# Order of the eight sampling matmuls in a deformable-convolution network: group by group instead of half by half

## The chip, the cores and the metric

The kernel runs on one core of a Trainium2 chip. The metric is device time in microseconds (us) of one execution of the whole program, four convolution layers over a batch of four images. The runs of the kernel before took 7743.75, 7739.45 and 7736.22 us, with a median of 7739.45 us.

## The reference, cut to what matters

The input is a tensor of 4 images, 256 channels, 64 x 64 pixels, in 32-bit floats. Four layers follow one another, each a group normalisation, a block, and a residual sum. The change lies in the first layer, a deformable convolution. There every pixel and every one of 4 channel groups (64 channels each) has 9 sampling points, whose places come from the data. Each point reads four neighbouring pixels (the corners) and weighs them bilinearly, and a softmax over the 9 points weighs the points:

```python
return tap(x0, y0, (1 - wx) * (1 - wy)) + tap(x0 + 1, y0, wx * (1 - wy)) + tap(x0, y0 + 1, (1 - wx) * wy) + tap(x0 + 1, y0 + 1, wx * wy)
...
samp = _grid_sample(img, sg)
mr = mask.reshape(n, H * W, G, P).transpose(0, 2, 1, 3).reshape(n * G, 1, H * W, P)
dout = (samp * mr).sum(-1).reshape(n, G * GC, H * W).transpose(0, 2, 1).reshape(n, H, W, C)
dout = jnp.einsum('nhwc,oc->nhwo', dout, outproj_w) + outproj_b
```

So for each pixel and group, 36 weighted rows of 64 channels are added up (9 points, 4 corners), and the result goes through a 256 x 256 projection.

## The kernel before

**Stages.** `run` (line 1178) works image by image. While image n is sampled, other work of earlier images stands beside it: for image 0 the convolutions and offsets of the images after it, for image 1 the feed-forward part and the linear attention of image 0, for images 2 and 3 also the last two layers of images 0 and 1. The tail after the sampling finishes what is left. A helper, `beside` (line 1194), takes one sampling round at a time and then lets the other generators advance by their share of cost. Under `manual_schedule` (line 1217) PE, DVE, ACT and POOL execute their instructions in the order in which the Python code issues them, so this interleaving is the order on each engine's queue.

**A sampling round.** `sample` (line 556) walks an image in rounds of 14 pixels (`RP`), with 9 points each, so that 126 of 128 partitions are points; there are 293 rounds an image and 1172 in all. A table in memory, `tab`, holds for each group and place a row of 64 channels for two lines, so that 256 consecutive floats give all four corners of a point: two halves of 128 floats, one for each x, and in each half two corners of 64 channels.

- `gathered` (line 596) allocates `g`, a tile of 128 partitions x 4 groups x 256 floats with 7 buffers. POOL issues four indirect DMAs (line 600), one for each group, which fetch 128 rows of 256 floats by the indices in `sl`.
- Eight matmuls follow (lines 605 to 608). For group i and half x the stationary operand is a slice of `wm` with 32 columns (2 corners x 16 pixel slots) and the moving operand is the half of `g` with 128 columns. The result goes to partitions 32i to 32i+31 of `acc` in PSUM, so each group has 32 columns of the PE array and 32 PSUM partitions to itself. The half x=0 starts the sum and the half x=1 is added to it.
- `weigh` (line 585) makes `wm` for four rounds on DVE, from weights and a mask that has each point's pixel.
- Two rounds share a half of the `acc` bank. When both are done, `moved` (line 610, ACT) copies it to SBUF, `turned` (line 614, PE) transposes it, and `spread` (line 619, ACT) writes it to `dT`. At the end of a block of 16 rounds come `project` (line 636, PE), `add` (DVE) and `finish` (ACT). They are held in `later` and issued some rounds afterwards, ahead of that round's own gathers and matmuls.

The first matmul of each group waits for that group's gather; the first of a round waits also for `wm` and for the copy that frees `acc`. The last matmul of a round tells the others that the round is done: POOL, which reuses the `g` buffer seven rounds later, ACT for `acc`, and DVE for `wm`.

**Another place with column tiles.** In the first image's convolution, `projected` (lines 385 to 393) also writes parts of PSUM's partitions: its loop over h chooses partitions 0 to 63 or 64 to 127, and the loop over the two contraction halves k stands inside it (line 392).

Of the kernel before, what the change touches and what calls it, by code (L numbers as in the profile page):

```python
# [23 lines left out]
G, PT = 4, 9  # L24
# [47 lines left out]
class Net:  # L72
# [483 lines left out]
    def sample(self, n, ssum):  # L556
# [39 lines left out]
        def gathered(sl, wm, acc, r):  # L596
            r4, acc = r % WR, acc[:, r % UR * P:(r % UR + 1) * P]
            g = self.gp.tile([P, G, 256], F32, name="g", bufs=7)
            for i in range(G):
                nc.gpsimd.indirect_dma_start(  # L600
                    out=g[:, i, :], out_offset=None, in_=table,
                    in_offset=bass.IndirectOffsetOnAxis(ap=sl.bitcast(I32)[:, r, i:i + 1], axis=0))


            for x in range(2):
                for i in range(G):
                    nc.tensor.matmul(acc[32 * i:32 * i + 32, :], wm[:, r4, 4 * i + 2 * x:4 * i + 2 * x + 2, :],  # L607
                                     g[:, i, x * P:(x + 1) * P], start=x == 0, stop=x == 1)

# [47 lines left out]
        for i, (b, r) in enumerate(order):  # L657
            for f in later.pop(i, ()):
                f()
            sl, rounds = blocks[b]  # L660
            if r % UR == 0:
                acc = next(accs)
            gathered(sl, wm, acc, r)
            if r == 0 and b + 1 < len(BLOCKS):
                load(b + 1)
            ends = r + 1 == len(rounds)
            if r % WR == 0:
                if r + WR < len(rounds):
                    nxt = weigh(b, r + WR)
                elif b + 1 < len(BLOCKS):  # L670
                    nxt = weigh(b + 1, 0)
            if r % UR == UR - 1 or ends:
                unit = rounds[r - r % UR:r + 1]
                todo = [partial(moved, acc, len(unit), i), partial(turned, len(unit), i), partial(spread, unit, b, i)]

                todo = [(i + 1 + j + (j == 2 and r < UR), f) for j, f in enumerate(todo)]
                if ends:
                    todo += [(i + 4 + m + j, partial(f, b, m)) for m in range(KT) for j, f in enumerate((project, add, finish))]
                for j, f in todo:
                    later.setdefault(j, []).append(f)  # L680
            if r % WR == WR - 1 or ends:
                wm = nxt
            yield 1
# [659 lines left out]
```

## Time and profile before

| What | us |
|---|---|
| median of the runs | 7739.45 |
| span of the profiled execution | 8805.8 |
| of this: before the first sampling round | 139 |
| sampling of the four images (1172 rounds) | 7192 |
| after the last sampling round | 1475 |
| PE busy with matmuls | 5993.9 |
| DVE busy | 5173.3 |
| POOL busy | 5152.4 |
| ACT busy | 2183.8 |
| matmuls of line 607, busy in all | 1034.8 |

The profiled execution has a longer span than the runs without a profile took. PE is TensorE (matmuls), PEld its weight loads, DVE is VectorE, ACT ScalarE, POOL GpSimd. A row of the profile that groups instructions has the line of the kernel, the engine, the operation, the tiles written and read, the count, the busy time and the mean duration of one in ns, and the idle time of the engine ahead of them with what ended it. A matmul in 32-bit floats appears as two array instructions, each with a weight load. Matmuls overlap, so the busy time of a group is the time in which at least one of them ran, and not the count times the mean. In a row of a stretch, the columns are the stretch, its length, the busy time of PE, PEld, DVE, ACT and POOL with instruction counts, the granted share of the TensorE clock, the share of the DMA engines and GB/s.

### The profile page before, as it was taken

How to read it: one execution, taken by the hardware profiler on the slowest of the kernel's cores; microseconds unless marked ns; L12 is line 12 of the kernel's file. 1: busy time of each engine (PE TensorE's matmuls, PEld its weight loads, DVE VectorE, ACT ScalarE, POOL GpSimd, SP SyncE). 2: the span in 40 equal slices, each digit the busy share in tenths (PEclk: the TensorE clock that was granted, in tenths of full speed). 3: DMA queues.
4: the chain of work that ended last, by engine and by line, in shares of the span. 5: the costliest groups of instructions: out<-in, count | busy, mean ns of one | idle time of the engine just before them, and what ended most of it. 6: DMA issues, size and time to landing. Idle time of an engine off the chain costs nothing. (4 is left out here: it accounts for less than half of the span.)

```text
span 8805.8 us, 95736 instructions
## 1 busy us (share of the span) xinstructions
PE 5993.9 (68%) x36532; PEld 3575.6 (41%) x36532; DVE 5173.3 (59%) x6409; ACT 2183.8 (25%) x4899; POOL 5152.4 (59%) x4950
## 2 busy tenths in 40 slices
PE   4454554448744446688876677888766778986899
PEld 2222222224323322244544443345544433664477
DVE  5444443443466667424777776227777772599834
ACT  1111111112211112122223222222222222465524
POOL 2666666566666666666666656666666661376410
PEclk7676766669866667799988888898878888998999
DMA  6454454444433334444443344444434343220131
GB/s 172 127 155 124 141 154 118 125 145 145 153 105 105 110 105 129 127 130 138 134 135 110 112 121 136 142 134 132 136 115 117 114 118 99 69 74 29 48 98 53
DMA packets 759050, 1042.27 MB, mean 118 GB/s; under 512 B 362432, under 2 KB 472128, under 8 KB 757056
## 3 DMA queue, kind: packets, MB, share of 16 engines
q0 software_dynamic: 225024, 614.77, 24.3%
q1 hardware_dynamic: 533568, 421.39, 16.4%
q8 instruction: 289, 4.73, 0.2%
q14 instruction: 169, 1.38, 0.0%
HBM read 867.08 MB, written 168.69 MB: 118 GB/s over the span
## 5 line engine op out<-in xcount | busy, mean ns | idle before, releaser
L600 POOL DMA_INDIRECT g<-tab,sl x4688 | 4618.5, 985 | 2687.8 <-issue 1224.2
L178 DVE SCALAR_TENSOR_TENSOR agg<-pad,vec,agg 128x1024 f32<-128x1024 f32 x2280 | 2933.5, 1287 | 61.9
L607 PE MATMUL acc<-g,wm 128*32 128x128 f32 x18752 | 1034.8, 333 | 1907.8 <-ACT at L612 1273.7
L607 PEld LDWEIGHTS acc<-g,wm 128*32 128x32 f32 x18752 | 566.8, 128 | 2411.7 <-ACT at L612 1446.1
L1048 PE MATMUL ps<-xd,w 128*128 128x256 f32 x3072 | 752.7, 396 | 51.3 <-issue 37.8
L591 DVE TENSOR_TENSOR wm<-con,sl 128x1024 f32<-128x1024 f32 (+1 forms) x296 | 357.7, 1209 | 711.9 <-remote 533.5
L1048 PEld LDWEIGHTS ps<-xd,w 128*128 128x128 f32 x3072 | 595.1, 199 | 175.0 <-issue 86.0
L632 ACT COPY dT<-dp 64x112 f32<-64x112 f32 x1176 | 285.9, 243 | 1043.7 <-remote 544.3
L742 PE MATMUL ps<-x2f,f 128*128 128x512 f32 x1024 | 499.2, 636 | 19.1 <-issue 7.7
L817 PE MATMUL ps<-xr,qw 128*128 128x512 f32 x768 | 472.0, 746 | 22.1 <-issue 11.1
L727 DVE SCALAR_TENSOR_TENSOR hm<-ps,vec,lk 128x512 f32<-128x512 f32 x256 | 190.8, 750 | 492.9 <-ACT lk L744 405.5
L752 PE MATMUL ps<-hm,f 128*128 128x512 f32 x1024 | 467.1, 605 | 0.9 <-DVE hm L727 0.9
L612 ACT COPY at<-acc 128x256 f32<-128x256 f32 (+1 forms) x588 | 218.3, 371 | 986.3 <-remote 753.2
L999 POOL TENSOR_TENSOR xd<-xp 128x640 f32<-128x640 f32 x64 | 79.4, 1268 | 492.6 <-ACT xp L1011 298.3
L640 PE MATMUL po<-dT,ow 128*128 128x224 f32 (+1 forms) x1216 | 326.1, 419 | 45.4 <-issue 19.3
L617 PE MATMUL dp<-ident,at 128*128 128x128 f32 x1172 | 284.1, 330 | 106.6 <-ACT dT L632 61.0
L865 ACT COPY kt<-pt 128x512 f32<-128x512 f32 x256 | 149.4, 584 | 829.3 <-remote 403.8
L744 ACT ACTIVATE lk<-ps,low 128x512 f32<-128x512 f32 x256 | 174.0, 687 | 666.0 <-PE ps L742 512.1
L1147 PE MATMUL s<-ph,th 128*128 128x512 f32 x512 | 290.2, 672 | 62.5 <-ACT kt L865 15.9
L640 PEld LDWEIGHTS po<-dT,ow 128*128 128x128 f32 x1216 | 265.5, 233 | 113.8 <-issue 68.9
L1167 PEld LDWEIGHTS ps<-gt,pT 128*128 128x128 f32 x2048 | 276.0, 213 | 70.8 <-issue 46.1
L194 POOL TENSOR_TENSOR ak<-ak,m 128x1024 f32<-128x1024 f32 x96 | 228.1, 2376 | 130.6 <-ACT m L193 126.7
(243 smaller groups left out, 8022.0 us busy)
## 6 DMA issues: line engine op xcount, KB each, us to landing
g<-tab,sl POOLq DMA_INDIRECT x4688
x<-x SPq DMA_DIRECT2D x128, 512.0 KB
xr<-x SPq DMA_DIRECT2D x96, 512.0 KB
tab<-xo SPq DMA_DIRECT2D x192, 128.0 KB
x<-in_x SPq DMA_DIRECT2D x32, 512.0 KB
y<-yc SPq DMA_DIRECT2D x32, 512.0 KB
x2f<-x SPq DMA_DIRECT2D x32, 512.0 KB
xyf<-x SPq DMA_DIRECT2D x32, 512.0 KB
```

Of the source, the lines that this page charges most:

```text
L178: nc.vector.scalar_tensor_tensor(to, s, wt, acc, ALU.mult, ALU.add)
L591: nc.vector.tensor_tensor(wm[:, 0:nu], self.con("own").unsqueeze(1).unsqueeze(1).to_broadcast(sh), sl[:, r:r + nu, G:].unsqueeze(3).to_bro ...
L600: nc.gpsimd.indirect_dma_start(out=g[:, i, :], out_offset=None, in_=table, in_offset=bass.IndirectOffsetOnAxis(ap=sl.bitcast(I32)[:, r, i: ...
L607: nc.tensor.matmul(acc[32 * i:32 * i + 32, :], wm[:, r4, 4 * i + 2 * x:4 * i + 2 * x + 2, :], g[:, i, x * P:(x + 1) * P], start=x == 0, st ...
L617: nc.tensor.transpose(dp[u][:, v].rearrange("p g s o -> p (g s o)"), at[u][:, v], self.ident)
L632: nc.scalar.copy(dT[b][hs, :, q0:q0 + m * (v1 - v0)].rearrange("p g (v o) -> p g v o", o=m), dp[u][hs, v0:v1, :, s, 0:m].rearrange("p v g ...
L640: nc.tensor.matmul(po[m][:, 0:np_], self.ow[:, k, m * P:(m + 1) * P], dT[b][:, k, 0:np_], start=k == 0, stop=k == G - 1)
L742: nc.tensor.matmul(ps, f1[:, k, m * P:(m + 1) * P], x2[:, k], start=k == 0, stop=k == KT - 1)
L752: nc.tensor.matmul(ps, f2[:, k, m * P:(m + 1) * P], hm[:, k], start=k == 0, stop=k == 4 * KT - 1)
L817: nc.tensor.matmul(ps, qw[:, k, m * P:(m + 1) * P], x[:, k], start=k == 0, stop=k == KT - 1)
L1048: nc.tensor.matmul(ps[:, e], w[:, k, t, 2 * half + e, m * P:(m + 1) * P], v[:, 2 * half + e, k, t:t + 8], start=i % 6 == 0, stop=i % 6 == 5)
L1147: nc.tensor.matmul(s[i], tv[:, 4 * b + j], ph[:, i * 512:(i + 1) * 512], start=True, stop=True)
```

## The change

The two loops around the eight matmuls of a round change places. Before, the four groups' first halves are issued and then the four groups' second halves; now both halves of group 0 are issued, then both of group 1, and so on. Operands, destinations and the start and stop flags stay as they are, and so do the gathers ahead of the loops.

```diff
-            for x in range(2):
-                for i in range(G):
+            for i in range(G):
+                for x in range(2):
                     nc.tensor.matmul(acc[32 * i:32 * i + 32, :], wm[:, r4, 4 * i + 2 * x:4 * i + 2 * x + 2, :],
                                      g[:, i, x * P:(x + 1) * P], start=x == 0, stop=x == 1)
```

## The prediction

> **What bounds the kernel now.** I read the span and clock first, then the stretches by image, the costliest groups, and the matmuls of line 607 one by one.
>
> ```profile
> core 0: 8805.8 us, clock 0.809
> ```
>
> The profiled execution took 8805.8 us, 1066.4 us (14%) more than the median of the runs shown, 7739.45. Part of the surplus can be seen: there are stretches in which no arithmetic engine works, such as this one, the columns being PE, PEld, DVE, ACT and POOL.
>
> ```profile
> 990.90:1001.00 10.10, 0.00 (x0) 0.00 (x0) 0.00 (x0) 0.00 (x0) 6.45 (x7) 0.65 0.45 133
> ```
>
> Such holes are no part of the change, so I use the profile for durations of single instructions and add the result to the median; I don't scale it by the span.
>
> The sampling of the four images fills 139 to 7331 us. By image:
>
> ```profile
> 139.00:1913.00 1774.00, 839.98 (x6645) 481.31 (x6646) 782.49 (x1036) 248.35 (x689) 1162.29 (x1170) 0.66 0.48 137
> 1913.00:3667.00 1754.00, 1036.69 (x6813) 547.54 (x6814) 1053.20 (x1056) 339.92 (x869) 1160.62 (x1172) 0.74 0.42 123
> 3667.00:5487.00 1820.00, 1367.42 (x8673) 819.04 (x8672) 1147.21 (x1372) 453.97 (x1108) 1144.32 (x1172) 0.87 0.44 128
> 5487.00:7331.00 1844.00, 1387.29 (x8814) 827.11 (x8813) 1153.10 (x1382) 459.89 (x1121) 1147.28 (x1172) 0.86 0.43 125
> ```
>
> PE is busy 47, 59, 75 and 75% of an image, DVE 44 to 63%, yet all four images take nearly the same time. What they share is POOL: 1172 gathers each.
>
> ```profile
> L600 POOL DMA_INDIRECT g<-tab,sl x4688 | 4618.5, 985 | 2687.8 <-issue 1224.2
> L607 PE MATMUL acc<-g,wm 128*32 128x128 f32 x18752 | 1034.8, 333 | 1907.8 <-ACT at L612 1273.7
> POOL g L600 <- PE acc L607: 494.3, 201, 23.2
> ```
>
> A gather starts 1.25 us after the one before (0.95 us and 0.30 of issue in the timeline), so a round of four needs 5.0 us of POOL. The 1172 rounds take 7192/1172 = 6.1 us each in the profile. If only the sampling were shorter in the unprofiled runs, it would be (7739.45 - 139 - 1475)/1172 = 5.2 us, an estimate that puts POOL at its pace nearly throughout. PE is the nearest second: 1387/293 = 4.7 us a round in the last image. So PE's time in a round counts in part: where POOL waits for PE to free a buffer (494 us), or where all wait behind PE's queue.
>
> **The round itself.** 18752/1172 = 16 array instructions for 8 matmuls, two for each. Counts of matmuls begun in one burst, by windows that end at 4005.572, .579, .586, .592, .704, .706 and 4006.10:
>
> ```profile
> L607 PE MATMUL acc<-g,wm x1: 297/297/297, 4005.6 to 4005.6; 128*32 128x128 f32 x1
> L607 PE MATMUL acc<-g,wm x2: 297/297/297, 4005.6 to 4005.6; 128*32 128x128 f32 x2
> L607 PE MATMUL acc<-g,wm x3: 297/297/297, 4005.6 to 4005.6; 128*32 128x128 f32 x3
> L607 PE MATMUL acc<-g,wm x4: 297/297/297, 4005.6 to 4005.6; 128*32 128x128 f32 x4
> L607 PE MATMUL acc<-g,wm x5: 272/297/297, 4005.6 to 4005.7; 128*32 128x128 f32 x5
> L607 PE MATMUL acc<-g,wm x16: 272/273/297, 4005.6 to 4005.9; 128*32 128x128 f32 x16
> ```
>
> Four begin within 20 ns, 7 ns apart; then nothing begins until 134 ns after the first. So the four groups run side by side on their 32 columns in four waves. Whether that survives the new order is the whole question.
>
> The kernel has a line where neighbours already share their columns: line 392 in `projected`, part of the first image's convolution, whose loops (388 to 392) put k innermost. Two matmuls, hence four array instructions, go to columns 0 to 63 before the first one for columns 64 to 127. If a matmul waited for all before it, the second column half would begin about three waves late. One burst of it, in windows from 955.44 that end at 955.453 and .466 (the one to .464 still has one matmul, the one to .4515 none), and in the timeline:
>
> ```profile
> L392 PE MATMUL ps<-iw,yc x1: 430/430/430, 955.5 to 955.5; 128*64 128x256 f32 x1
> L392 PE MATMUL ps<-iw,yc x2: 430/430/430, 955.5 to 955.5; 128*64 128x256 f32 x2
> ...
> 955.45 2.00 PE L392 MATMUL ps<-iw,yc 128*64 128x256 f32 x16
> ```
>
> The first two begin 11 to 14.5 ns apart, I take 13, and all 16 take 2.00 us where one alone is recorded with 0.38 to 0.43: they go in pairs from the first wave on. The array works off its column tiles independently, whatever stands between them in the program. The 13 ns are two matmuls at 6.7 ns, the same 6.7 ns that one matmul costs between groups on line 607.
>
> **What the Trainium skill says.** "TensorE: Matmul & The Clock Gate", Part 3, The mechanism, says that matmuls on different array tiles overlap with about 4 ns between starts; here it is 7 ns for a matmul of two instructions, of the same size. It also says that matmuls start and end strictly in program order. Line 392 doesn't agree: in strict order its second column half could not begin 13 ns after the first. "TensorEngine Tiling (Array Packing)", Key Properties, says that tiles operate independently and that a change of tiling mode drains the array; the first fits line 392, and the second the timeline, where the 128x512 matmul after the burst begins at 4006.14, 0.57 us after the burst's start and only after its last wave. The table at the top of the first page gives TensorE a queue of 64; a round has 32 instructions, loads counted. No trace here shows that limit.
>
> **The change, part by part.** Removed and added: nothing; the same 9376 matmuls with the same operands, flags and accumulation per group.
>
> Moved: matmul (group 1, half 0) goes from second to third place, group 2 from third to fifth, group 3 from fourth to seventh; the second halves move forward. No DMA, no queue but PE's. Within a column tile the order is the same as before, so a tile's own chain stays: starts at 0, 134, 243, 352 ns (the waves at 109 ns after the first).
>
> Cost: the four tiles begin one matmul apart now (0, 7, 13, 20 ns) and two matmuls apart after (0, 13, 27, 40 ns), by line 392's 13 ns. The last tile ends 20 ns later, and the next 128-row work waits for it. 1172 x 20 ns = 23.4 us on PE's queue. Two rounds without PE work in between might pay a little more, since a tile's queue is then full when the next group comes; I put that at under 2 us in all.
>
> The gather waits sit on each group's first matmul. A late group 3 leaves four instructions in its tile after its landing, 352 ns to the last start, before and after; groups 0 to 2 would have more behind them. PE waits for landings 46 us in 49 cases, so a gain is bounded by about 49 x 0.25 = 12 us (two waves each, an estimate) and is near nothing, since the tiles run in parallel anyway. The evacuation (ACT, line 612) and POOL wait for the round's end alone: 20 ns later.
>
> How much of the 23.4 us shows: at most PE's share of the images, (0.47 + 0.59 + 0.75 + 0.75)/4 = 0.64, giving 15 us, or all of it if PE's queue sets the pace in unprofiled runs, 23; at least what POOL waits for line 607, 494/7192 = 0.07, 2 us. What hides the rest is POOL's 5.0 us a round; were it gone, all 23 would show. I take 0.4, between 0.07 and 0.64 and nearer the upper since the last two images are so close to both limits: +9.4 us, 7739.45 + 9.4 = 7749, +0.12%.
>
> **Rivals.** About 0.2% (15.5 us) is what a measurement of this kernel can tell from no change.
>
> *A shared hold-back (slower).* In line 392 the pairs are even for four waves only; what holds in a queue of two 64-column tiles needn't hold for four tiles of 32. If the array holds back only some eight instructions for all tiles together, three waiting for each of groups 0 and 1 and two for group 2 fill it, and group 3 begins a wave late: about 115 ns a round, 1172 x 0.115 = 135 us on PE. It decides from the point where PE's round passes POOL's; with the same 0.4: +54 us, 7793. For it: it is not excluded. Against it: line 607 itself has at least seven waiting after the first wave, and a shared store weighted by columns would be odd.
>
> *Strict order (slower).* Only the last of a group's four instructions overlaps the next group: last start at 4 x 352 + 3 x 7 = 1429 ns against 372, +1.06 us a round, 1239 us on PE. Images 3 and 4 then need 4.7 + 1.06 = 5.8 us a round of PE against 5.2; with half of it showing +620 us, 8360. Line 392 speaks against it.
>
> *Earlier start of the second halves (faster).* Worth at most the 12 us above, 7734 with half of it. More than 0.2% would need the engines' phases to shift favourably too.
>
> **How the numbers follow.** The lag case has 0.74 (0.42 within 0.2%, 0.29 slower since the lag may show in full or with a few us of shifted phases on top, 0.03 faster); the shared hold-back 0.10 (0.09 slower, 0.01 within); strict order 0.06, slower; the earlier start 0.10 (0.06 faster, 0.04 within). So faster 0.09, same 0.47, slower 0.44. The likeliest case alone spans 7735 to 7765 (0 to 23 us, and the 4 us by which the runs before stray). The range reaches down to 7728 for the earlier start and up to 7795 for the shared hold-back; strict order and the far tails are left out.
>
> **What would show it.** Right: in the changed kernel's burst the first wave begins at 0, 13, 27, 40 ns, the last start is 392 ns after the first instead of 372, line 607's PE busy time grows by about 20 us, and rounds, waits and clock are otherwise the same. Group 3's first start at 130 ns or more speaks for the shared hold-back; a burst of over 1.4 us for strict order. Wrong in its second half: bursts as foretold, but the time off by over 25 us, which would put the cause outside the array.

## The result and the profile after

The changed kernel took 7768.87 us (median of 7 runs, 7761.36 to 7771.16), the kernel before 7744.24 us (7 runs, 7736.22 to 7747.75): ratio 1.003, interval 1.002 to 1.004, or 24.6 us more. The forecast was 7749.0 with a range of 7728 to 7795. So the time lies in the range, on the slower side, 19.9 us over the forecast.

The first profile of the kernel before, on which the prediction rests, has a span of 8805.8 us. Later runs on one chip, called chip 13 here, take about 8830 us for this program instead of 7740; the first profile has such a time, and stretches in which no arithmetic engine works (halts). Which chip it came from is not known. The profile after has a span without that surplus, so it must be set beside an execution of the kernel before on a chip that shows none (chip 9, `before_null` below). The page of the changed kernel, with its span and three of the costliest groups of the sampling:

```profile
span 7768.7 us, 95736 instructions
...
L600 POOL DMA_INDIRECT g<-tab,sl x4688 | 4610.9, 984 | 1667.7 <-issue 1316.2
...
L607 PE MATMUL acc<-g,wm 128*32 128x128 f32 x18752 | 1507.9, 310 | 1025.7 <-ACT at L612 513.0
...
L591 DVE TENSOR_TENSOR wm<-con,sl 128x1024 f32<-128x1024 f32 (+1 forms) x296 | 357.5, 1208 | 404.3 <-PE acc L607 385.9
```

The same page of the kernel before, on chip 9:

```profile
span 7735.2 us, 95736 instructions
...
L600 POOL DMA_INDIRECT g<-tab,sl x4688 | 4594.5, 980 | 1652.0 <-issue 1311.6
...
L607 PE MATMUL acc<-g,wm 128*32 128x128 f32 x18752 | 1323.0, 319 | 1106.2 <-DMA g<-tab,sl 575.1
```

Two things are to be seen. POOL's gathers, which the change doesn't touch, are busy 16.4 us longer in all, and POOL's idle time before them grew by 15.7 us; together that is the 33.5 us between these two spans, to within 2 us. What grew in the idle time is POOL's wait for the matmuls of line 607 to free a `g` buffer: 116.0 us in 96 waits in the kernel before, 133.5 us in 100 waits in the changed one. And the matmuls of line 607 are busy 184.9 us longer, not the 20 that were foretold. In the kernel before, PE's largest wait ahead of them is for landing gathers (575.1 us), of which the first profile showed 46.

The burst itself is as foretold. Counts of matmuls begun in one burst of the changed kernel, whose first start is at 4007.994 us, in windows that end at 4008.003, .0125, .0400, .1350 and .3900 (the window to .1200 still has four):

```profile
L607 PE MATMUL acc<-g,wm x1: 297/297/297, 4008.0 to 4008.0; 128*32 128x128 f32 x1
L607 PE MATMUL acc<-g,wm x2: 297/297/297, 4008.0 to 4008.0; 128*32 128x128 f32 x2
L607 PE MATMUL acc<-g,wm x4: 297/297/297, 4008.0 to 4008.0; 128*32 128x128 f32 x4
L607 PE MATMUL acc<-g,wm x5: 273/297/297, 4008.0 to 4008.1; 128*32 128x128 f32 x5
L607 PE MATMUL acc<-g,wm x16: 272/273/297, 4008.0 to 4008.4; 128*32 128x128 f32 x16
```

Read at full resolution, the sixteen begin at 0, 14, 27, 40, then 134, 147, 160, 174, 243 and so on to 392 ns. Four groups run side by side in four waves, two matmuls' issue apart: the lag of 20 ns at the end is there. The question is whether it is what costs 24.6 us; 1172 rounds of 20 ns would be 23.4 us, nearly the same.

### The profile page after: what moved, and what is told of

The parts are those of the page before. It is cut to its first block, busy times and chain, and to the rows that moved or that the text cites. A ratio compares the mean times of both kernels' runs of the same rounds, so it can differ in the third digit from the quotient of the medians.

```text
span 7768.7 us, 95736 instructions
## 1 busy us (share of the span) xinstructions
PE 6126.8 (79%) x36532; PEld 3735.2 (48%) x36532; DVE 5164.4 (66%) x6409; ACT 2187.4 (28%) x4899; POOL 5144.8 (66%) x4950
## 5 line engine op out<-in xcount | busy, mean ns | idle before, releaser
L600 POOL DMA_INDIRECT g<-tab,sl x4688 | 4610.9, 984 | 1667.7 <-issue 1316.2
L607 PE MATMUL acc<-g,wm 128*32 128x128 f32 x18752 | 1507.9, 310 | 1025.7 <-ACT at L612 513.0
L607 PEld LDWEIGHTS acc<-g,wm 128*32 128x32 f32 x18752 | 878.1, 120 | 1689.6 <-ACT at L612 725.7
L1048 PE MATMUL ps<-xd,w 128*128 128x256 f32 x3072 | 708.8, 383 | 7.5 <-DVE x L1028 3.3
L1048 PEld LDWEIGHTS ps<-xd,w 128*128 128x128 f32 x3072 | 574.6, 192 | 108.4 <-issue 30.3
L742 PE MATMUL ps<-x2f,f 128*128 128x512 f32 x1024 | 482.4, 619 | 4.2 <-ACT f L717 3.9
L817 PE MATMUL ps<-xr,qw 128*128 128x512 f32 x768 | 445.6, 711 | 21.5 <-issue 7.5
L617 PE MATMUL dp<-ident,at 128*128 128x128 f32 x1172 | 263.3, 310 | 69.8 <-ACT dT L632 69.7
L640 PE MATMUL po<-dT,ow 128*128 128x224 f32 (+1 forms) x1216 | 287.1, 386 | 23.3 <-DVE yb L644 11.4
L742 PEld LDWEIGHTS ps<-x2f,f 128*128 128x128 f32 x1024 | 192.3, 195 | 232.7 <-issue 220.1
L752 PEld LDWEIGHTS ps<-hm,f 128*128 128x128 f32 x1024 | 188.4, 190 | 223.9 <-issue 222.4
```

Of the source, the lines that this page charges most:

```text
L600: nc.gpsimd.indirect_dma_start(out=g[:, i, :], out_offset=None, in_=table, in_offset=bass.IndirectOffsetOnAxis(ap=sl.bitcast(I32)[:, r, i: ...
L617: nc.tensor.transpose(dp[u][:, v].rearrange("p g s o -> p (g s o)"), at[u][:, v], self.ident)
L640: nc.tensor.matmul(po[m][:, 0:np_], self.ow[:, k, m * P:(m + 1) * P], dT[b][:, k, 0:np_], start=k == 0, stop=k == G - 1)
L742: nc.tensor.matmul(ps, f1[:, k, m * P:(m + 1) * P], x2[:, k], start=k == 0, stop=k == KT - 1)
L752: nc.tensor.matmul(ps, f2[:, k, m * P:(m + 1) * P], hm[:, k], start=k == 0, stop=k == 4 * KT - 1)
L817: nc.tensor.matmul(ps, qw[:, k, m * P:(m + 1) * P], x[:, k], start=k == 0, stop=k == KT - 1)
```

## The experiments

Two theories stood at first. *Lag*: PE's queue is 20 ns later a round, and part of it shows. *Order of landing*: the cost comes in the rounds in which PE waits for gathers. Such rounds are nearly all in the first two images, while PE is busiest in the last two. So the order was changed in some images only, beside fresh runs of the kernel before.

### The kernel before again (chip 13)

No edit; two runs, one with each of the next two sets.

> The kernel before once more, for an undisturbed profile: a span of about 7742 us beside 7744 us of time. All theories expect bursts of line 607 with first starts at 0, 7, 13, 20 ns and a last start at 372 ns. If POOL sets the pace of images 0 and 1, their bursts wait for landings (as the profile of the changed kernel shows) and those images take the same time as there, to 5 us; if PE's queue sets the pace of images 2 and 3, these are shorter here by 10 to 25 us.

> The kernel before a third time, to read it beside the profile of the changed kernel (7768.7 us). If this chip gives 7744 us: images 0 and 1 wait for landings in some 210 and 140 rounds as there, and last as long as there (1521 and 1533 us, to 5 us); images 2 and 3 are shorter by 10 to 12 us in all if only their 586 rounds show 20 ns each, and all four are shorter by about 6 us each if every round shows it. If this chip gives 8830 us: image lengths of about 1800 us as in the last look.

8834.59 and 8806.52 us. On this chip the kernel before has medians of 8829.73 and 8824.11 us in the two sets. The first profile (8805.8) is of this kind. What is compared on chip 13 therefore has some 1090 us of other time in it.

### The new order in two of the four images (chip 13)

```diff
-            for x in range(2):
-                for i in range(G):
+            for i, x in [(i, x) for i in range(G) for x in range(2)] if n < 2 else [(i, x) for x in range(2) for i in range(G)]:
```

This is `first_images`; `last_images` has `n > 1` instead of `n < 2`. `first_again` and `last_again` repeat them.

> Group order in the sampling of images 0 and 1 only, the order of before in images 2 and 3. Lag on PE's queue in every round alike: half of the change, +12 us (7756). Lag that shows only where PE doesn't wait for gathers: images 0 and 1 wait for them in most rounds, so 0 to +5 us (7744 to 7749). A cost that arises while PE waits inside a burst for a gather, and not from the lag: nearly all of it here, +20 to +25 us (7767).

> Group order in images 2 and 3 only. Lag in every round alike: +12 us (7756). Lag that shows only where PE doesn't wait for gathers: 586 rounds x 20 ns = 12 us from the array, and nearly the whole 24.6 us of the change if it has no other place, so +12 to +25 us. A cost of waits inside bursts: 0 to +5 us.

> Group order in images 0 and 1 only, again, for a chip without the long halts. Lag in every round alike: +12 us over the kernel before. Lag only where PE doesn't wait for gathers: 0 to +5 us. A cost of waits inside bursts: +20 to +25 us.

> Group order in images 2 and 3 only, again. Lag in every round alike: +12 us. Lag only where PE doesn't wait for gathers: +12 us, and up to +25 us if the 24.6 us of the change all lie here. A cost of waits inside bursts: 0 to +5 us.

Ratios to the kernel before: first images 0.9992 (0.9984 to 1.0) and 1.0004 (0.9993 to 1.0015); last images 1.001 (0.9999 to 1.0021) and 1.0002 (0.999 to 1.0014). The repeats don't confirm the first pair, and all four are within 0.1% of no change. For the first images the intervals allow -14 to 0 and -6 to +13 us, so the 20 to 25 us expected of a cost that arises in waits did not show on this chip. That says little of the other chip: in `before_third` only 49 rounds of images 0 and 1 have starts over more than 1 us, against 334 in `before_null`, so the rounds in which PE waits for landings are nearly absent here. The changed kernel itself was not run on chip 13.

### Groups in pairs (chip 13)

```diff
-            for x in range(2):
-                for i in range(G):
+            for i, x in [(i, x) for h in (0, 2) for x in range(2) for i in (h, h + 1)]:
```

> Groups 0 and 1 half by half, then groups 2 and 3 half by half. If a start costs one matmul's issue (6.7 ns) for each matmul ahead of it in the program, the first starts of the four groups are at 0, 7, 27 and 33 ns and the last start at 385 ns, 13 ns later than before; the time is then 13/20 of the change's, +16 us (7760). If a shared queue or the array's program order held anything back, group 2 would start a wave (110 ns) late and the time would be over +60 us. A cost of waits inside bursts alone has no reason to follow 13/20.

Ratio 1.0012 (1.0002 to 1.0022), about 2 to 19 us more. In the bursts without a wait the first starts of the groups are at 0, 7, 27 and 33 ns and the last start is at 385 ns (medians), as 6.7 ns for each matmul ahead in the program give. The model of the burst holds for a third order. The time agrees with the 16 us that the lag was expected to cost, but doesn't single it out.

### Two rounds' matmuls issued together (chip 13)

If PE's queue sets the pace, one change of tile shape fewer in each pair of rounds should show. The matmuls of two rounds that share a half of `acc` are issued after the second round's gathers, in the old order:

```diff
-            gathered(sl, wm, acc, r)
+            held.append((gathered(sl, r), wm, acc, r))
...
+                while held:
+                    sampled(*held.pop(0))
```

The last two lines stand where the half of `acc` is full or the block of rounds ends; `sampled` has the two loops of before.

> The order of before within a round, but the matmuls of the two rounds that share an acc half are issued together after the second round's gathers, so that PE changes between 128x32 and 128x128 half as often. In the profile of the changed kernel a change costs 93 ns on the way in (522 against 429 ns between starts) and 94 ns on the way out (203 against 109): 187 ns saved for about 470 pairs that were apart. If PE's queue sets the pace in every image: -88 us. If only in images 2 and 3: about -44 us. If POOL set the pace of all images, as the prediction held for the rest of the lag: 0, or some us more since a g buffer comes free a round later.

Ratio 1.0088 (1.0068 to 1.0107), about 81 us slower, where the expectation had at most some us more. In the trace the first round's sixteen begin in their waves, but the last seven of the second round's begin at 892 to 1515 ns (medians), where 808 ns had been expected for the last of all. Most of them come late in images 0 and 1; in images 2 and 3 only the last few do. POOL's waits for these matmuls to free a `g` buffer are 637.1 us, against 494.3 in the first profile. So PE's saving can't be told from what the later release and the halts cost. The next runs are on chip 9.

### The changed kernel, and eight instructions a tile in a row (chip 9)

`after_here` is the changed kernel. `merged_groups` is `merged` with the loops turned round, so that all eight array instructions of a column tile (two rounds, two halves, two each) stand together in the program:

```diff
+        def sampled(todo):
+            for i in range(G):
+                for g, wm, acc, r in todo:
+                    r4, to = r % WR, acc[:, r % UR * P:(r % UR + 1) * P]
+                    for x in range(2):
+                        nc.tensor.matmul(to[32 * i:32 * i + 32, :], ...
```

> The changed kernel on the chip of the other experiments, whose executions take some 1090 us more, with halts in which PE issues nothing. Lag on PE's queue showing in full whatever else halts PE: +23 us over the kernel before here too (ratio 1.0027). If the halts (a late supply of PE's instructions) set the pace, part of the lag falls into them: less than half of it, ratio 1.000 to 1.0013. First starts at 0, 13, 27, 40 ns in either case.

> Both rounds of an acc half together, and group by group over both: eight array instructions in a row for one column tile. If each column tile takes one running and three waiting instructions of its own, and the program stops at the first that finds its tile full: the eighth of group 0 gets in when the fifth starts, so group 1 first starts at 461 to 470 ns, group 2 at about 930 and group 3 at about 1395, and a pair of rounds ends about 2180 ns after its first start, against 808 in the half-by-half order of the merged kernel. If eight waiting instructions are shared by all tiles: group 1 starts at 27 ns. If matmuls overlapped only with the next in the program: group 1 at about 800 ns. Time: over 350 us more than the merged kernel if PE's queue sets the pace (8905 us there).

`after_here`: 7756.87 us against 7739.27, ratio 1.0023 (1.0014 to 1.0032), 17.6 us. Its expectation was written for the chip with the halts, but the run fell on chip 9. The loss is there again; whether the first result came from this chip is not known.

`merged_groups`: 7742.13 us, ratio 1.0004 (0.9998 to 1.0011), 2.9 us. One of its bursts, first start at 4007.018 us, counts in windows that end at 4007.0200, .4700, .4800, .4868 and 4009.30:

```profile
L609 PE MATMUL acc<-g,wm x1: 297/297/297, 4007.0 to 4007.0; 128*32 128x128 f32 x1
L609 PE MATMUL acc<-g,wm x4: 272/273/297, 4007.0 to 4007.4; 128*32 128x128 f32 x4
L609 PE MATMUL acc<-g,wm x5: 272/273/297, 4007.0 to 4007.5; 128*32 128x128 f32 x5
L609 PE MATMUL acc<-g,wm x6: 272/273/297, 4007.0 to 4007.5; 128*32 128x128 f32 x6
L609 PE MATMUL acc<-g,wm x32: 272/273/297, 4007.0 to 4009.2; 128*32 128x128 f32 x32
```

The counts don't name the group; the pattern of the starts does. Up to 351 ns only group 0 runs, four instructions of it. Its fifth begins at 461 ns, and group 1's first at 466; group 2's first follows at 933, group 3's at 1400, and the last start of all is at 2188 ns. The 317 bursts of this run that no wait spreads have medians within 1 ns of these. So group 1 can issue when group 0 has one instruction running and three waiting. The starts fit a store of its own for each column tile: when it is full, all that is behind it in the program waits. With four instructions to a tile, as in the changed kernel, no start is held back.

The last start comes 2188 ns after the first, where the old order would have 808 by the same waves, and PE's busy time shows it. Rows of stretches: stretch, length, busy time of PE, PEld, DVE, ACT and POOL with counts, granted clock, DMA share, GB/s. The four images of the kernel before (`before_null`):

```profile
139.00:1660.00 1521.00, 999.24 (x6754) 528.38 (x6758) 801.57 (x1067) 251.93 (x699) 1156.28 (x1176) 0.71 0.56 160
1660.00:3190.00 1530.00, 1123.93 (x6896) 565.23 (x6896) 1045.86 (x1047) 349.37 (x888) 1162.43 (x1184) 0.79 0.49 144
3190.00:4730.00 1540.00, 1264.91 (x8669) 774.59 (x8669) 1142.00 (x1372) 455.06 (x1108) 1146.75 (x1173) 0.91 0.52 152
4730.00:6270.00 1540.00, 1262.02 (x8653) 771.23 (x8653) 1138.98 (x1368) 455.02 (x1108) 1125.97 (x1154) 0.91 0.51 148
```

and the last two images of `merged_groups`:

```profile
3190.00:4730.00 1540.00, 1383.87 (x8668) 965.16 (x8667) 1141.56 (x1372) 451.85 (x1108) 1142.94 (x1172) 0.95 0.52 151
4730.00:6270.00 1540.00, 1380.63 (x8644) 962.99 (x8645) 1141.77 (x1372) 450.66 (x1106) 1143.38 (x1170) 0.95 0.51 148
```

PE is busy 119 us longer in each of the two images in which it is busiest, and from the last burst of one image to the last of the next these images take 1541.0 and 1543.2 us, against 1541.1 and 1542.8 before. PE has nearly that much room in these images: half the changes of tile shape fall away as well, which by the price given at the end is at most 27 us an image (an estimate, 146 x 0.187). The 20 ns of lag are 5.9 us an image (293 rounds) of the same kind of time. The expectation that a PE-bound queue would cost some 350 us falls, and with it the lag as a cause in images 2 and 3. It is not settled for images 0 and 1, which take 15.7 us longer in this execution than in `before_null`.

### The kernel before against itself, and the last images again (chip 9)

`before_null` has no edit. `last_third` is the edit of `last_images`.

> The kernel before, timed against itself: a ratio of 1.000 with 1 inside its interval of about 0.1% to either side; anything else would be a cost of the loading of a program and not of its order. On a chip without the halts its profile shows where the changed kernel's 18 to 25 us lie: in images 2 and 3 if the lag shows where POOL waits for PE (each 6 to 10 us shorter than the 1542 us there, images 0 and 1 alike), spread over all four if it shows in every round; in POOL's own time if the gathers beside DVE take less long (the surplus over 946 ns a gather sums to 174 us in the changed kernel).

> Group order in images 2 and 3 only, for a chip without the halts (on the other one both halves of the change lay within 0.1%). Lag that shows where POOL waits for PE: nearly all of the change, +15 to +20 us beside the +17.6 us of the changed kernel there. Lag in every round alike: +9 us. A cost that arises while PE waits for landings, in images 0 and 1: 0 to +4 us.

`before_null`: ratio 1.0001 (0.9993 to 1.0009). `last_third`: 7743.57 against 7737.91 us, ratio 1.0006 (0.9999 to 1.0013), 5.7 us, under the 15 to 20 us of a lag that shows where POOL waits for PE. The interval, -1 to +10 us, holds both other expectations: the 9 us of a lag that shows in every round alike, and 0 to 4 us for a cost in images 0 and 1. By difference to 17.6, some 12 us belong to the first two images, with an uncertainty of about 9 us (an estimate from the two intervals); those weren't timed alone on chip 9. No run shows a kernel faster than the one before by more than its interval.

## Where the time went

The two stretches of `after_here` to be laid beside the first two rows of `before_null` above:

```profile
139.00:1660.00 1521.00, 1072.08 (x6726) 646.67 (x6726) 796.61 (x1056) 249.79 (x693) 1159.31 (x1170) 0.78 0.55 159
1660.00:3190.00 1530.00, 1145.18 (x6883) 619.79 (x6884) 1045.39 (x1046) 345.92 (x879) 1157.00 (x1179) 0.85 0.48 142
```

POOL gets through six and five instructions fewer in the same stretches (1176 to 1170, 1184 to 1179), with PE busier (by 73 and 21 us) and its clock higher (0.71 to 0.78, 0.79 to 0.85). Here POOL's gathers follow one another nearly without a wait for PE, and PE waits for landings, in some 345 of the 586 rounds in `before_null`. In the old order all second halves stand behind the first half of group 3, so PE does most of a round after the last landing. In the new order it does both halves of each group as it lands. So PE waits less for landings ahead of line 607 (496.7 us against 575.1), and less is left to do at the end.

"TensorE: Matmul & The Clock Gate", Part 1, of the Trainium skill says that the array runs at half its clock until it has been busy, and at full clock after that. The traces fit in the main. Of the rounds whose starts spread over more than 1 us, 215 of 334 have their last two waves about 213 ns apart in the old order; in the new one 202 of 358 have about 109 ns.

What a sooner end of the burst can do is seen in the timeline. One round of image 1 in `before_null` (start, duration, engine, line and operation, and in brackets the idle time before it and what ended it):

```profile
2309.56 1.06 PE L607 MATMUL acc<-g,wm 128*32 128x128 f32 x10 [0.80 <-DMA g<-tab,sl]
2310.55 0.94 POOL L600 DMA_INDIRECT g<-tab,sl  x1 [0.30 <-issue]
...
2310.66 1.23 DVE L591 TENSOR_TENSOR wm<-con,sl 128x1024 f32<-128x1024 f32 x1 [3.09 <-PE acc L607]
...
2311.80 0.95 POOL L600 DMA_INDIRECT g<-tab,sl  x1 [0.31 <-issue]
```

and the same round in `after_here`, from one gather earlier:

```profile
2313.94 2.62 DVE L178 SCALAR_TENSOR_TENSOR agg<-pad,vec,agg 128x1024 f32<-128x1024 f32 x2
2314.45 0.95 POOL L600 DMA_INDIRECT g<-tab,sl  x1 [0.30 <-issue]
...
2316.95 0.94 POOL L600 DMA_INDIRECT g<-tab,sl  x1 [0.30 <-issue]
...
2317.18 0.62 PE L607 MATMUL acc<-g,wm 128*32 128x128 f32 x4 [0.58 <-DMA g<-tab,sl]
...
2317.84 1.23 DVE L591 TENSOR_TENSOR wm<-con,sl 128x1024 f32<-128x1024 f32 x1 [1.29 <-PE acc L607]
...
2318.20 1.69 POOL L600 DMA_INDIRECT g<-tab,sl  x1 [0.30 <-issue]
```

In the old order ten instructions remain after the last landing and take 1.06 us; DVE's `wm` for later rounds, which waits for the burst to free its buffer, begins 0.11 us after a gather has begun. That gather takes 0.94 us, the next 0.95. In the new order four remain and take 0.62 us, `wm` begins 0.36 us *before* the next gather, and that gather takes 1.69 us, 0.75 us more. The gather at 2314.45, beside products of line 178 that read their running sum from PSUM, takes 0.95 us.

"SBUF — State Buffer", Who interferes with whom, says that a DVE instruction with two SBUF inputs contends with a GpSimd instruction that reads SBUF, and that the order of issue decides who blocks. `wm` has two such inputs and the gather reads its indices from SBUF; the two timelines agree, 0.94 us against 1.69. The same section reports that a `tensor_tensor` did not stall DMAs, and infers that issuing them needs the write side; here one does hold back a gather, so the measurement decides.

The same can be counted over the traces. The lengthening is the time above 946 ns of all gathers of images 0 and 1 that overlap a `wm`. The two columns of counts say how long after the start of the last gather a `wm` of these images began (148 in all): shortly after it, or shortly before the next, since a gather starts each 1.25 us. The waits are POOL's waits for the bursts to free a `g` buffer, in the whole execution.

| Profiled execution | images 0 and 1, us | images 2 and 3, us | gathers busy, all images, us | POOL's waits for bursts, us | lengthening in images 0 and 1, us | `wm` 0 to 250 ns after | `wm` 750 to 1250 ns after |
|---|---|---|---|---|---|---|---|
| `before_null` | 3030.6 | 3083.9 | 4594.5 | 116.0 | 58.0 | 50 | 55 |
| `after_here` | 3046.9 | 3084.8 | 4606.2 | 121.2 | 71.5 | 36 | 75 |
| changed kernel, first profile | 3053.9 | 3091.5 | 4610.9 | 133.5 | 77.5 | 29 | 82 |
| `last_third` | 3037.6 | 3090.9 | 4601.2 | 124.3 | 65.7 | 38 | 64 |
| `merged_groups` | 3046.3 | 3084.2 | 4598.5 | 139.7 | 67.8 | 48 | 64 |

The counts shift from the first kind to the second in the changed kernel. A `wm` of the first kind lengthens gathers by 10 to 34 ns on average in these executions, one of the second kind by 757 to 826 ns. The lengthening beside `wm` grew by 13.5 us in `after_here` and by 19.5 in the first profile of the changed kernel. Other gathers took a little less, so that all gathers of images 0 and 1 took 8.9 and 15.2 us longer, of the 16.3 and 23.3 us by which these images are longer.

The rest has a second source. In images 0 and 1 POOL's waits for bursts grew by 5.0 and 8.9 us. Two of them, 2.0 and 3.4 us long, ahead of the gathers of rounds 46 and 61 of image 1 (counted from 0), stand in both profiles of the changed kernel, and in neither `before_null` nor `last_third`, which have the old order there. Before each of them PE works off line 742 at a lower granted clock. In `after_here` a block of twelve takes 7.11 us instead of 5.42 (clock 0.76 against 1.00 in `before_null`), and later a block of eight takes 5.40 instead of 3.70.

This has limits. It is a reading of five executions, each up to 9 us from its kernel's median (`after_here` was profiled at 7749.44 us with a median of 7756.87, `last_third` at 7752.33 with 7743.57). In `last_third` the first two images have the old order, and still they are 7.0 us longer than in `before_null` and have 7.7 us more lengthening: two executions of the same order differ by a third to over a half of what is set down to the new one. In `merged_groups` all gathers of images 0 and 1 take 4.6 us longer and the waits for bursts 13.9, of 15.7 us, so there it is mostly the waits. No kernel was run in which `wm` alone was moved, so the collision is a likely part of the cause, the waits behind slower matmuls are another, and neither is shown by an intervention. Images 2 and 3 are 0.9 and 7.6 us longer in the changed kernel's two profiles and 7.0 in `last_third`; the two longer ones go with 8.6 and 5.8 us more of POOL's waits for bursts there, and why the first has no such growth is open.

## Why the prediction was right and wrong

- **Four waves, one matmul's issue later for each group.** Right: 0, 14, 27, 40 ns and 392 ns at the end. The rule from line 392, 6.7 ns for each matmul ahead, also gave the starts of `pairs` to the nanosecond.
- **The rivals in the array.** Both are refuted: group 3 begins at 40 ns and not a wave late, and a burst takes 392 ns to its last start and not 1.4 us. `merged_groups` fits a store of four instructions for each column tile instead of a shared one.
- **The share of 0.4.** The reason given for it failed. It was set "nearer the upper since the last two images are so close to both limits". In those images 119 us more of busy PE cost nothing that shows. The lower bound came from 494 us that POOL waited for line 607 in the first profile; `before_null` has 116.0 us in 96 waits. POOL's waits did grow in the changed kernel, by 5.2 and 17.5 us in its two profiles, but in part through the slower matmuls of line 742 and not through 20 ns a round. For the last two images alone the measured cost is not resolved from zero. So it is in good part luck that the result lies in the range: gathers that take longer, which the forecast put at nothing, add 11.7 us where the spans differ by 12.5, and 16.4 where they differ by 33.5.
- **The gain of an earlier start, "bounded by about 49 x 0.25 = 12 us" and "near nothing, since the tiles run in parallel anyway".** This failed too. Without halts PE is short of gathers in some 345 rounds, where the first profile had 49 waits, and in these the second halves do start sooner. The burst does end sooner after the last landing, as that rival had it. But no gain came of it: the time rose, and what is released sooner, `wm`, falls more often just ahead of a gather.
- **"Rounds, waits and clock are otherwise the same", PE busy 20 us longer.** Wrong for the whole: 184.9 us longer, and the clock at 0.878 against 0.85. Right where PE doesn't wait for landings: in `after_here` line 607 is busy 5.4 and 5.7 us longer in images 2 and 3, as 293 rounds of 20 ns give, and 109 and 59 us longer in images 0 and 1, where PE works on the halves while it waits.
- **The holes are no part of the change, so durations are taken and spans are not.** Right for durations (0.95 us for a gather, 109 ns for a wave), but waits and counts of waits are no durations: they came from the disturbed profile all the same.
- **"the time off by over 25 us, which would put the cause outside the array".** The time is off by 19.9 us, less than that sign asks for. Still, what the traces show of the loss lies mostly outside the burst: in gathers that take longer and in waits of POOL.

## What to carry to other kernels

Here an earlier end of a burst on an engine with room to spare gained nothing; ask what its end releases and where that falls in the cycle of the engine that sets the pace. Small matmuls on separate column tiles ran side by side in all three orders with at most four instructions in a row for a tile, with 20 ns between the best and the worst; with eight in a row they did not. Before waits are read from a profile, set its span beside the runs without one: here the durations survived the disturbance, and the waits didn't (494 us against 116).

## What the hardware showed beyond expectation

- A gather of 0.95 us took 1.69 us when a DVE product of two SBUF tensors (1.23 us) had begun 0.36 us before it, and 0.94 us when the product began 0.11 us after it. In `before_null` the gathers that begin during a product of line 178, with one input in PSUM, take 946 ns on average.
- The starts fit one running and three waiting instructions for each 32-column tile. More for the same tile kept back all later ones, whatever tile they were for: with eight in a row group 1 began at 466 ns in `merged_groups`, where with four in a row it began at 14.
- A change to 32-column tiles and back costs some 93 and 94 ns, an estimate from the changed kernel's first profile: the starts on the two sides of it are 522 ns apart where 429 is the pace before, and 203 where 109 is the pace between waves.
- Two chips took 7740 and 8830 us for the same program.
